# GpSimd's sums behind the last softmax scaling, and the upper half of the scores first, in a graph-network kernel

## The chip, the core and the metric

The kernel runs on one core of one Trainium2 chip. The metric is device time in microseconds (us) of one execution: the median of three runs of the kernel before is 2493.54 us (2493.31 to 2493.93). All data are float32.

The engines are named as in the profile: PE multiplies matrices, DVE (VectorE) and ACT (ScalarE) work element by element, POOL (GpSimd) adds and subtracts whole tiles here, SP issues most of the DMAs. PSUM has eight banks of 128 x 512 float32, into which PE writes.

## The reference, cut to what matters

A graph convolution stands ahead of four transformer layers, and another behind them. The change touches the attention of layers 1 to 3 alone (layers are counted from 0):

```python
xb = xf.reshape(BS, n // BS, d)                      # 16 graphs of 64 nodes, d = 512
q = (xb @ Wq).reshape(BS, -1, H, DH)                 # 8 heads of 64
k = (cond @ Wk).reshape(BS, -1, H, DH)               # 256 keys for each graph
v = (cond @ Wv).reshape(BS, -1, H, DH)
att = jnp.einsum('bnhd,bmhd->bhnm', q, k) * DH ** (-0.5)
w = jax.nn.softmax(att, axis=-1)
o = jnp.einsum('bhnm,bmhd->bnhd', w, v).reshape(BS, -1, H * DH)
...
u = _ln(h, ln3_w[i], ln3_b[i]) @ geglu_w[i] + geglu_b[i]
val, gate = jnp.split(u, 2, axis=-1)
f = val * jax.nn.gelu(gate, approximate=False)
```

## The kernel before, in words

**Products in seven parts.** Each large product is split in 2 x 2 blocks and made from seven block products instead of eight (Strassen's scheme in Winograd's form). It needs sums and differences of blocks of both factors; where these are of weights or inputs they are made on POOL: `sums_of_a`, `sums_of_b` (L213 to L223) and `inner_right` (L969). A PE product then reads a sum as it would read the block.

**Steps.** The attention of a layer goes in eight steps, g = 0 to 7, of two graphs (128 rows) each. In step g the scores of that step are made (`scores`, L755): 16 matmul calls fill four PSUM banks, two for each half `c2` of the heads, a bank holding two heads for each of `a` = 0, 1. Then, for each bank u, DVE takes the row maximum (L774), ACT the exponentials with their sum (L779), DVE the reciprocal (L782) and two in-place scalings of 128 x 256 (L784): eight scalings a step, and `scores.last` is the last of them. While this goes on, PE makes the values of the next step (`values`, L744, by `seven`, L711: products pa, pb, pc, pd, then pa, pc, pd again, whose banks DVE and ACT empty at L722 to L738). Then `mix` (L789) transposes the scaled probabilities (L813), copies them to SBUF as pT (L816 on DVE, L818 on ACT) and multiplies them by the values (L802, bank po).

**Joint keys.** In layers 1 to 3 the keys of steps g + 1 and g + 2 are made together at the end of the odd steps g = 1, 3, 5 (`KeyPair`, L1102). This is a seven-part product whose parts are partly seven-part products again. For the inner ones, `cond_rights` (L1149) makes 16 differences of 128 x 256 on POOL (L973, tiles kr): four for each of four inner products, and the first seven-part product on PE (`seven_of`, L992) reads the first eight, the second one the last eight. `KeyPair.run` writes the keys' four tiles: those of the upper half of the heads (`kT(1, a)`) by DVE in `upper` and `lower` (L1141, L1144), those of the lower half by ACT, in `first` and, behind the very last products, in `final` (L1147). Behind the joint keys comes `scores` of step g + 1, which is even: it takes c2 = 0, the lower half, first.

**First gate weights.** In step 6 of layers 1 to 3 (`g == NG - 2`) POOL makes the four sums of 128 x 1024 for the first quarter of the gated projection (`geglu_weights`, L900; tiles ges, wgate; L220 to L223). Six row blocks of the next normalised input are also turned in this step: 24 transposes tr_ln on PE, whose results DVE (L698) and ACT (L700) scale into place.

**What sets the order.** Each engine takes its instructions in the order of the program; a scheduling layer has made this order and the waits between engines from what each tile is written and read by. `waiting_for(ins, engine)` (L60) adds one more wait: every instruction that is traced inside, on that engine, also waits for `ins`. The sums of the joint keys (L1499) have no such wait: they start when their DMAs have landed and POOL has come to them. The first gate weights of layers 1 to 3 (L1511) wait for `scaled.last`, which is the last normalisation on DVE (L172, tile xn_ln), ahead of the step's scores.

PSUM banks and SBUF tiles are given out in rotation; a bank's new writer waits for its last reader.

Of the kernel before, what the change touches and what calls it, by code (L numbers as in the profile page):

```python
# [23 lines left out]
def gnn_kernel(  # L24
# [67 lines left out]
    def bank(name):  # L92
        return psum.tile([P, 512], F32, tag="bank", name=name)

    def t512(name, dtype=F32):
        return work.tile([P, 512], dtype, tag="t512", name=name)
# [658 lines left out]
    def scores(l, g, qT, kT):  # L755


        c0 = (g % 4) * P
        probs = []
        banks = [bank(f"sc_{l}_{g}_{u}") for u in range(4)]  # L760
        for c2 in range(2):
            for a in range(2):
                for j in range(2):
                    pj = slice(j * DH, (j + 1) * DH)
                    for b in range(2):
                        with tc.issue_after(mix.last.ins) if g else nullcontext():
                            nc.tensor.matmul(  # L767
                                banks[2 * c2 + j][b * NPG:(b + 1) * NPG, a * M:(a + 1) * M],
                                qT[g // 4][c2][pj, a, c0 + b * NPG:c0 + (b + 1) * NPG],
                                kT(c2, a)[pj, b * M:(b + 1) * M], start=True, stop=True)  # L770
        for u in range(4):
            ps3 = banks[u].rearrange("p (a m) -> p a m", a=2)
            nmax = small.tile([P, 2], F32, tag="nmax", name=f"nmax_{l}_{g}_{u}")
            nc.vector.tensor_reduce(nmax, ps3, AX.X, OP.max, negate=True)  # L774
            pr = t512(f"pr_{l}_{g}_{u}")
            pr3 = pr.rearrange("p (a m) -> p a m", a=2)
            tot = small.tile([P, 2], F32, tag="tot", name=f"tot_{l}_{g}_{u}")
            for a in range(2):
                nc.scalar.activation(pr3[:, a, :], ps3[:, a, :], AF.Exp,  # L779
                                     bias=nmax[:, a:a + 1], accum_out=tot[:, a:a + 1])  # L780
            inv = small.tile([P, 2], F32, tag="inv", name=f"inv_{l}_{g}_{u}")
            nc.vector.reciprocal(inv, tot)  # L782
            for a in range(2):
                scores.last = nc.vector.tensor_scalar(pr3[:, a, :], pr3[:, a, :], inv[:, a:a + 1],  # L784
                                                      None, OP.mult)
            probs.append(pr)
        return probs

    def mix(l, g, probs, v, between=lambda: None):  # L789

        oT = t512(f"oT_{l}_{g}")
        po = bank(f"po_{l}_{g}")

        def weigh(c2, pTs):
            for a in range(2):
                c = 2 * c2 + a
                for b in range(2):
                    for m in range(MB):
                        for j in range(2):
                            n0 = c * P + b * NPG  # L800
                            at = (a * MB + m) * P + b * NPG
                            mix.last = nc.tensor.matmul(  # L802
                                po[j * DH:(j + 1) * DH, n0:n0 + NPG],
                                v[b][:, m, c * P + j * DH:c * P + (j + 1) * DH],
                                pTs[j][:, at:at + NPG],
                                start=(m == 0), stop=(m == MB - 1))

        last = None
        for c2 in range(2):
            pTs = []  # L810
            for j in range(2):
                u = 2 * c2 + j
                pt = transposed(probs[u], f"pr_{l}_{g}_{u}")  # L813
                pT = t512(f"pT_{l}_{g}_{u}")
                if j:
                    nc.vector.tensor_copy(pT, pt)  # L816
                else:
                    nc.scalar.copy(pT, pt)  # L818
                pTs.append(pT)
            if last is not None:  # L820
                between()
                weigh(*last)
            last = (c2, pTs)
        weigh(*last)
        nc.vector.tensor_copy(oT, po)
        return oT
# [322 lines left out]
    def cond_rights(l, g):  # L1149

        rooms = slots_of(4, f"kr_{l}_{g}")
        of = conds[l, g], conds[l, g + 1]
        return {i: inner_right(nc.gpsimd, *(x[i][:, k, :] for k in range(2) for x in of), room)
                for i, room in zip(INNER[0] + INNER[1], rooms)}
# [206 lines left out]
    for l in range(L):  # L1361
# [109 lines left out]
        for g in range(NG - 1):  # L1471
            if g == NG - 2:
                if l:
                    take_ln3()
                raw = load_geglu(l, 0)
            if l == 0:
                fetch_cond(g + 2)
            probs = scores(l, g, qT, kTs.pop(g))
            ready = [g - 2, g - 1] if g == NG - 2 else [g - 2] if g > 1 and not l else []

            def between(last_key):
                nonlocal left
                if len(oTs) == 2:
                    blocks = pair_sums(l, g - 2, oTs)
                    oTs.clear()
                    if g == NG - 2:
                        with waiting_for(scores.last, mybir.EngineType.Pool):
                            left = geglu_weights(l, 0, *raw)
                    for _ in attn_out_pair(g - 2, *blocks, wo7,
                                           *(bank(f"{x}_{l}_{g}") for x in ("wab", "wcd"))):  # L1490
                        pass
                ln3_norm(*ready, behind=last_key)
                for nb in ready:
                    add_bias(nb)

            if g in (1, 2):
                fetch_x(2 * l + g - 1)
            if l and g % 2:
                key_rights = cond_rights(l, g + 1)  # L1499

                def kept_moments(ins):
                    if g > 1:
                        with tc.issue_after(ins.ins):
                            moments_into(mv_kept[:, 2 * (g - 3):2 * (g - 1)], [h[g - 3], h[g - 2]],
                                         f"ln3_{l}_{g - 3}")

                vs[g + 1] = values(l, g + 1, wv, beside=kept_moments)
            elif l and g:
                turned = range(g) if g == NG - 2 else []
                if turned:  # L1510
                    with waiting_for(scaled.last, mybir.EngineType.Pool):  # L1511
                        left = geglu_weights(l, 0, *raw)
                vs[g + 1] = values(l, g + 1, wv, late=lambda: [ln3_turn(nb) for nb in turned])
                next_cond(l, g + 2)
                next_cond(l, g + 3)
            else:
                if g or l:
                    kT, vs[g + 1] = kv(l, g + 1, wk, wv, between,
                                       late=lambda: [ln3_turn(nb) for nb in ready])
                else:  # L1520
                    kT, vs[1] = kT_1, values(0, 1, wv)
                kTs[g + 1] = whole(kT)
                save_conds()
                next_cond(l, g + 2)
                if l:
                    next_cond(l, g + 3)
                    spare.append(rows.tile([P, D], F32, tag="last", name=f"spare_{l}"))
                    wk_lefts = inner_lefts(wk, [x[:, i * P:(i + 1) * P] for x in spare
                                                for i in range(4)])
            if g in (1, 2):  # L1530
                base_of(2 * l + g - 1)
            for nb in ready:
                if nb >= 4:
                    ln3_sums(nc.gpsimd, nb)
            oTs.append(mix(l, g, probs, vs.pop(g)))
            if l and g % 2:
                blocks = pair_sums(l, g - 1, oTs)
                oTs.clear()
                pair = KeyPair(l, g + 1, wk, wk_lefts, key_rights, (conds[l, g + 1], conds[l, g + 2]))
                pair.run(scale_kept if g == NG - 3 else lambda: None,  # L1540
                         lambda *banks: attn_out_pair(g - 1, *blocks, wo7, *banks,
                                                      tc.keep_in_program_order))
                if g == NG - 3:
                    ln3_norm(g - 1, g)
                kTs.update({g + 1 + n: pair.of(n) for n in range(2)})
        oT, = oTs
        g = NG - 1
        kT, v = kTs[g], vs[g]
        fT, fS, quads = quads_of(l, 0, left, right)
        probs = scores(l, g, qT, kT)  # L1550
# [133 lines left out]
```

## Time and profile before

| | |
|---|---|
| median of three runs | 2493.54 us |
| the profiled execution | 2493.92 us |
| its span, first to last instruction of the program | 2492.1 us |
| PE busy | 2460.9 us |
| DVE busy | 1574.9 us |
| ACT busy | 691.6 us |
| POOL busy | 807.4 us |
| DMA queue q1, share of 16 engines | 19.0% |

All times inside the program are read against the span, and 1.8 us of the profiled execution lie outside it. A row of the timeline has the start and the duration in us, the engine, the line, the operation, out<-in by the tiles' names, the shape and a count of merged instructions; in brackets stands the idle time of the engine before it and what ended it. The view of stretches has, for each stretch, its length, then for each engine the busy time and in brackets the number of instructions, then PE's granted clock. The view of one line has the minimum, median and maximum duration in ns. PE's ends are modelled and its matmuls overlap, so a step's length is taken from the start of its scores to the start of the next step's.

### The profile page before, as it was taken

The numbers are of one execution on the slowest core, as the hardware profiler recorded it, in microseconds if no ns is written. First come the engines' busy times: TensorE is split into PE (matmuls) and PEld (weight loads), VectorE is DVE, ScalarE is ACT, GpSimd is POOL, SyncE is SP. The second block draws the span as 40 slices with busy tenths as digits, with TensorE's granted clock in tenths as the row PEclk, the third lists the DMA queues.
The fourth block names the chain that finished last, engine by engine and source line by source line (L and its number), as shares of the span: only waits on it lengthen the run. The fifth ranks groups of instructions, "written<-read, shape, count | busy, mean of one in ns | idle before, by whom it ended". The sixth has DMA issues, their size and how long they took to land. (4 is left out here: it accounts for less than half of the span.)

```text
span 2492.1 us, 33980 instructions
## 1 busy us (share of the span) xinstructions
PE 2460.9 (99%) x12968; PEld 1869.3 (75%) x12968; DVE 1574.9 (63%) x3199; ACT 691.6 (28%) x1564; POOL 807.4 (32%) x883
## 2 busy tenths in 40 slices
PE   8999999999999999999999999999999999999999
PEld 5778886677778887577787888477787888577775
DVE  9655665666765657666675667666684566666661
ACT  7322222122213334122212333222222333322221
POOL 0322223632422222532542223344523141444410
PEclk9999999999999999999999999999999999999999
DMA  6313222110312211111212222011121121111110
GB/s 177 132 39 107 98 92 87 51 39 13 102 30 81 94 64 55 39 43 34 98 34 73 73 77 69 23 45 51 34 97 68 40 96 52 51 51 51 51 68 35
DMA packets 70395, 162.97 MB, mean 65 GB/s; under 512 B 5880, under 2 KB 6208, under 8 KB 70224
## 3 DMA queue, kind: packets, MB, share of 16 engines
q1 hardware_dynamic: 68128, 155.28, 19.0%
q0 software_dynamic: 1376, 4.30, 0.5%
q8 instruction: 107, 1.75, 0.3%
q10 hardware_dynamic: 720, 1.11, 0.1%
q14 instruction: 64, 0.52, 0.1%
HBM read 137.60 MB, written 23.07 MB: 64 GB/s over the span
## 5 line engine op out<-in xcount | busy, mean ns | idle before, releaser
L220 POOL TENSOR_TENSOR ges<-wgate,wgate 128x1024 f32<-128x1024 f32 x16 | 37.6, 2352 | 420.8 <-DVE fs L1175 401.3
L779 ACT ACTIVATE pr<-sc,nmax 128x256 f32<-128x256 f32 x256 | 118.0, 474 | 173.7 <-DVE nmax L774 173.7
L302 PE MATMUL pa_v<-wv,ct 128*128 128x256 f32 x512 | 123.8, 384 | 1.7 <-ACT s_v L722 1.7
L302 PE MATMUL pc_v<-wv,ct 128*128 128x256 f32 x512 | 121.6, 380 | 2.6 <-DVE u_v L728 2.4
L302 PE MATMUL fa<-wff,fT 128*128 128x256 f32 x512 | 121.6, 379 | 0.0
L302 PE MATMUL pd_v<-wvs,ct 128*128 128x256 f32 x512 | 121.0, 379 | 0.0
L784 DVE TENSOR_SCALAR pr<-pr,inv 128x256 f32<-128x256 f32 x256 | 115.8, 494 | 2.8
L302 PEld LDWEIGHTS fa<-wff,fT 128*128 128x128 f32 x512 | 97.3, 190 | 21.8 <-issue 9.6
L302 PEld LDWEIGHTS pa_v<-wv,ct 128*128 128x128 f32 x512 | 95.4, 190 | 22.2 <-issue 6.2
L302 PEld LDWEIGHTS pc_v<-wv,ct 128*128 128x128 f32 x512 | 96.2, 190 | 17.5 <-DVE u_v L728 5.0
L1009 ACT COPY gs<-ga 128x512 f32<-128x512 f32 x48 | 27.9, 582 | 287.7 <-PE ga L1002 287.7
L302 PEld LDWEIGHTS pd_v<-wvs,ct 128*128 128x128 f32 x512 | 97.3, 190 | 13.2
L302 PE MATMUL ga<-ln3T,wval 128*128 128x512 f32 x224 | 104.4, 594 | 0.0
L774 DVE TENSOR_REDUCE nmax<-sc 128x2 f32<-128x512 f32 x128 | 82.9, 678 | 33.3 <-PE sc L767 33.3
L1083 ACT ACTIVATE g<-g,gcols 128x512 f32<-128x512 f32 x96 | 69.3, 722 | 94.8 <-DVE g L1080 94.8
L1210 DVE TENSOR_TENSOR hall<-fd,hall 128x512 f32<-128x512 f32 x64 | 44.1, 689 | 54.1 <-PE fd L302 54.1
L1428 POOL TENSOR_TENSOR hall<-hall,ffb 128x512 f32<-128x512 f32 x32 | 40.1, 1276 | 117.5 <-DVE fs L1175 71.2
L302 PE MATMUL gc<-ln3S,wgate 128*128 128x512 f32 x160 | 75.2, 592 | 0.0
L802 PEld LDWEIGHTS po<-pT,v 128*64 128x64 f32 x2048 | 62.9, 138 | 11.7 <-issue 7.2
L802 PE MATMUL po<-pT,v 128*64 128x64 f32 x2048 | 67.7, 224 | 3.5 <-DVE pT L816 3.5
L1210 DVE TENSOR_TENSOR hall<-fc,hall 128x512 f32<-128x512 f32 x64 | 44.0, 687 | 41.6 <-PE fc L302 41.6
L302 PEld LDWEIGHTS ga<-ln3T,wval 128*128 128x128 f32 x224 | 41.3, 190 | 35.9 <-issue 34.4
(476 smaller groups left out, 6146.0 us busy)
## 6 DMA issues: line engine op xcount, KB each, us to landing
ct<-cond_dram SPq DMA_DIRECT2D x72, 512.0 KB, 5.5
wval<-in_L_gnn_geglu_w_dram SPq DMA_DIRECT2D x32, 512.0 KB, 3.8
wgate<-in_L_gnn_geglu_w_dram SPq DMA_DIRECT2D x32, 512.0 KB, 4.6
wff<-in_L_gnn_ffo_w_dram SPq DMA_DIRECT2D x32, 512.0 KB, 3.8
cond_dram<-ct SPq DMA_DIRECT2D x24, 512.0 KB, 3.0
cond<-in_L_gnn_cond_dram SPq DMA_DIRECT2D x32, 256.0 KB, 4.6
ct<-cond_dram SPq DMA_DIRECT2D x24, 256.0 KB, 5.7
wk<-in_L_gnn_Wk_dram SPq DMA_DIRECT2D x8, 512.0 KB, 4.3
```

What stands on the lines that cost most here:

```text
L220: t.tensor_tensor(s1, a21, a22, OP.add)
L302: each(nc.tensor.matmul(at, left[:, k, l0:l1], right[:, k, r0:r1], start=start and n == 0 and k == 0, stop=n == len(cols_of) - 1 and k == ...
L774: nc.vector.tensor_reduce(nmax, ps3, AX.X, OP.max, negate=True)
L779: nc.scalar.activation(pr3[:, a, :], ps3[:, a, :], AF.Exp, bias=nmax[:, a:a + 1], accum_out=tot[:, a:a + 1])
L784: scores.last = nc.vector.tensor_scalar(pr3[:, a, :], pr3[:, a, :], inv[:, a:a + 1], None, OP.mult)
L802: mix.last = nc.tensor.matmul(po[j * DH:(j + 1) * DH, n0:n0 + NPG], v[b][:, m, c * P + j * DH:c * P + (j + 1) * DH], pTs[j][:, at:at + NPG ...
L1009: nc.scalar.copy(s1, a)
L1083: nc.scalar.activation(g, g, AF.Gelu, bias=gate)
L1210: nc.vector.tensor_tensor(to, halves_of(of), to, OP.add)
L1428: nc.gpsimd.tensor_tensor(h[nb], h[nb], ffb, OP.add)
```

## The change

Three things are changed in layers 1 to 3, and nothing elsewhere. The sums for the joint keys wait, on POOL, for the step's last scaling of probabilities (`scores.last`). The sums for the first gate weights wait for it as well, in place of the last normalisation. And `scores` of steps 2, 4 and 6 takes the upper half of the heads first, in the matmuls, in the softmax behind them and in `mix`.

```diff
-        probs = []
+        probs = {}
         banks = [bank(f"sc_{l}_{g}_{u}") for u in range(4)]
-        for c2 in range(2):
+        halves = (1, 0) if l and g and g % 2 == 0 else (0, 1)
+        for c2 in halves:
             for a in range(2):
...
-        for u in range(4):
+        for u in (2 * c2 + j for c2 in halves for j in range(2)):
...
-            probs.append(pr)
+            probs[u] = pr
...
-        for c2 in range(2):
+        for c2 in dict.fromkeys(u // 2 for u in probs):
...
             if l and g % 2:
-                key_rights = cond_rights(l, g + 1)
+                with waiting_for(scores.last, mybir.EngineType.Pool):
+                    key_rights = cond_rights(l, g + 1)
...
                 if turned:
-                    with waiting_for(scaled.last, mybir.EngineType.Pool):
+                    with waiting_for(scores.last, mybir.EngineType.Pool):
                         left = geglu_weights(l, 0, *raw)
```

Line numbers in the text are those of the kernel before. In the built programs, the order on SP is the same in both. On POOL it is the same but for one pair of neighbours inside each set of 16 sums. On PE, DVE and ACT the halves of steps 2, 4 and 6 change places, and nothing else moves. No instruction is added or removed.

## The prediction

> **What bounds the kernel now.** I read the page's busy shares first, then PE's waits, then the durations of DVE's scalings, and last the lengths of the steps.
>
> ```profile
> PE 2460.9 (99%) x12968; PEld 1869.3 (75%) x12968; DVE 1574.9 (63%) x3199; ACT 691.6 (28%) x1564; POOL 807.4 (32%) x883
> PE po L802 <- DVE pT L816: 3.5, 3, 1.2
> PE tr_ln L184 <- DVE u_v L725: 2.7, 3, 0.9
> PE pc_v L302 <- DVE u_v L728: 2.4, 3, 0.9
> PE pa_v L302 <- ACT s_v L722: 1.7, 3, 0.6
> ```
>
> PE is busy in 2460.9 of 2492.1 us. As the change takes no matmul away, only PE's waits can be won, and what adds a wait to PE costs its full length. Four of its waits (total, times, longest) come three times each, once in each of layers 1 to 3, and all four end on work behind DVE's softmax. DVE is busy 63% overall, so something local holds it:
>
> ```profile
> L784 DVE TENSOR_SCALAR pr<-pr,inv x256: 336/349/2507, 177.4 to 2140.0; 128x256 f32<-128x256 f32 x128
> L784 DVE TENSOR_SCALAR pr<-pr,inv x8: 344/348/353, 828.3 to 831.2; 128x256 f32<-128x256 f32 x8
> L784 DVE TENSOR_SCALAR pr<-pr,inv x16: 342/809/885, 846.3 to 899.8; 128x256 f32<-128x256 f32 x16
> 960.55 2.71 DVE L784 TENSOR_SCALAR pr<-pr,inv 128x256 f32<-128x256 f32 x2
> 963.85 4.21 DVE L784 TENSOR_SCALAR pr<-pr,inv 128x256 f32<-128x256 f32 x2
> 969.41 0.68 DVE L725 TENSOR_TENSOR u_v<-pb_v,s_v 128x512 f32<-128x512 f32 x1
> 958.33 2.35 POOL L220 TENSOR_TENSOR ges<-wgate,wgate 128x1024 f32<-128x1024 f32 x1 [4.88 <-DVE xn_ln L172]
> 965.55 2.35 POOL L223 TENSOR_TENSOR ges<-wval,ges 128x1024 f32<-128x1024 f32 x1
> ```
>
> One scaling of 128 x 256 takes 349 ns by the median and up to 2507. In step 2 of layer 1 (from 824), where POOL does nothing, all eight lie within 344 to 353. In steps 3 and 4 (846 to 900) the median of 16 is 809 ns: there POOL's 0.73 us sums for the joint keys run beside them. In step 6 POOL's four gate sums run from 958.33 to 967.90, each 2.35 us, and a pair of scalings takes 2.71 or 4.21 us. So a scaling that falls beside POOL waits for about the rest of the sum that is running. The instructions behind it on DVE, u_v at 969.41 first, are late for PE.
>
> What that costs PE is the length of a step, from the first score to the next step's:
>
> ```profile
> 777.84:824.46 46.62, 46.62 (x305) 40.44 (x301) 26.64 (x50) 14.85 (x36) 7.81 (x11) 1.00 0.06 18
> 842.70:890.35 47.65, 46.88 (x304) 40.35 (x300) 29.95 (x52) 14.14 (x35) 19.29 (x28) 1.00 0.31 106
> 1419.45:1467.02 47.57, 46.89 (x304) 40.35 (x300) 29.87 (x52) 14.14 (x35) 19.30 (x28) 1.00 0.31 106
> 1996.12:2043.91 47.79, 46.89 (x305) 40.35 (x301) 30.09 (x52) 14.14 (x35) 19.31 (x28) 1.00 0.32 105
> 824.46:842.70 18.24, 18.24 (x170) 15.79 (x169) 11.07 (x25) 7.41 (x22) 0.00 (x0) 1.00 0.40 146
> 890.35:908.95 18.60, 18.51 (x169) 15.70 (x168) 12.50 (x23) 6.70 (x21) 9.17 (x13) 1.00 0.00 1
> 2043.91:2062.49 18.58, 18.50 (x169) 15.69 (x168) 12.48 (x23) 6.70 (x21) 9.15 (x13) 1.00 0.00 1
> 955.57:979.92 24.35, 21.72 (x194) 18.45 (x193) 21.58 (x46) 11.01 (x33) 14.41 (x12) 1.00 0.40 132
> 2109.11:2133.44 24.33, 21.71 (x194) 18.45 (x193) 21.57 (x46) 11.00 (x33) 14.39 (x12) 1.00 0.43 131
> ```
>
> The first row is step 1 of layer 1, whose sums ended before its scalings began; PE never pauses in it. Rows two to four are step 3 of layers 1 to 3: the same PE work in 47.57 to 47.79. Then step 2 (clean), step 4 of layers 1 and 3, and step 6 of layers 1 and 3. The granted clock is 1.00 throughout, so nothing here is throttling.
>
> **The change part by part.** *Key sums later.* The wait puts the 16 sums of an odd step behind its own eight scalings. Step 3 then has no POOL beside its softmax, nor has step 4, beside which the sums of step 5 ran. I take the clean steps as what is left:
> - step 3: 47.65, 47.57 and 47.79 less 46.62 is 1.03 + 0.95 + 1.17 = 3.15 us.
> - step 4: 18.60 less 18.24 is 0.36; with layer 3's 0.34, and layer 2 between, 3 x 0.35 = 1.05 us.
> - steps 1 and 5 are clean already: 0.
>
> *What the wait could make late.* Behind the sums on POOL stand only the four sums of pairs of outputs (L850 on), which wait for oT. PE reads the first eight key sums in kb.
>
> ```profile
> 784.10 0.62 DVE L784 TENSOR_SCALAR pr<-pr,inv 128x256 f32<-128x256 f32 x2
> 768.71 0.73 POOL L973 TENSOR_TENSOR kr<-ct,ct 128x256 f32<-128x256 f32 x1 [11.73 <-DMA ct<-cond_dram]
> 778.45 1.52 POOL L973 TENSOR_TENSOR kr<-ct,kr 128x256 f32<-128x256 f32 x2
> 796.72 0.72 POOL L850 TENSOR_TENSOR os<-oT 128x256 f32<-128x256 f32 x1 [16.75 <-DVE oT L825]
> 796.74 0.59 PE L1002 MATMUL kb<-kr,wks 128*128 128x256 f32 x2
> ```
>
> In step 1 the last scaling ends at 784.72. The 16 sums take 768.71 to 779.97 now, 11.3 us, so they will run from 784.7 to 796.0: 0.7 us ahead of L850's own start at 796.72. The first eight are done at about 790.4, 6.3 us before kb at 796.74. The other odd steps have the same distances once their softmax is clean, and DMAs that held the sums until now have landed before. So this costs nothing; no DMA is issued by POOL here, and SP's order is unchanged.
>
> *What the sums fall beside now.* Next on DVE are u_v, v, pT and oT, whose source is PSUM; they ran beside POOL before with no loss (below, the u_v of L728 never over 693 ns). Step 1 also has two additions from SBUF to SBUF:
>
> ```profile
> L728 DVE TENSOR_TENSOR u_v<-pc_v,u_v x32: 680/692/693, 134.8 to 2123.7; 128x512 f32<-128x512 f32 x32
> L1447 DVE TENSOR_TENSOR x_again<-x_again,bias_out x8: 679/681/1446, 213.6 to 1986.3; 128x512 f32<-128x512 f32 x8
> 787.35 0.68 DVE L730 TENSOR_TENSOR v<-pd_v,u_v 128x512 f32<-128x512 f32 x1
> 790.19 1.89 PE L302 MATMUL pd_v<-wvs,ct 128*128 128x256 f32 x8
> ```
>
> L1447 took 1446 ns once, against 681. If it and its neighbour L1448 each take that long, v (L730) ends at 788.03 + 1.53 = 789.56, and PE needs its bank at 790.19. I take 0; without that cover it would be 3 x 1.53 = 4.6 us. [...]
>
> *Gate sums later.* In step 6 the four sums will run behind the last scaling, at about 958.1 + 5.75 = 963.9 (5.75: step 1's first maximum at 778.97 to 784.72), until 973.5. They end before POOL's next work, at 974.77 now, and PE reads them only behind step 7. To see what the step takes without stalls, I add the 24 transposes tr_ln to the clean step 2:
>
> ```profile
> 773.98 1.91 PE L184 MATMUL tr_pr<-ident,pr 128*128 128x128 f32 x16
> 775.82 2.08 PE L802 MATMUL po<-pT,v 128*64 128x64 f32 x64
> 778.97 1.29 DVE L774 TENSOR_REDUCE nmax<-sc 128x2 f32<-128x512 f32 x2 [0.32 <-PE sc L767]
> 974.77 1.44 POOL L213 TENSOR_TENSOR ln3S<-ln3T,ln3T 128x256 f32<-128x256 f32 x2 [6.87 <-DVE ln3T L698]
> ```
>
> Sixteen transposes take 775.82 - 773.98 = 1.84 us, 24 take 2.76: 18.24 + 2.76 = 21.0, and 24.35 - 21.0 = 3.35 us a layer. The idle times agree: 0.6 + 0.9 + 1.2 = 2.7 us, and each pause costs some 0.26 more than its idle time (step 3: 47.65 less 46.62 is 1.03, of which 0.77 is idle by 47.65 less 46.88), 3.4 in all. I take 3 x 3.4 = 10.2 us. DVE turns its 12 halves tr_ln behind u_v and v. These start some 5.5 us sooner (963.9 against 969.41), while PE comes only 3 us sooner, so DVE's lateness should be gone.
>
> *Upper half first.* Behind the joint keys, PE's scores wait within themselves:
>
> ```profile
> 779.72 1.99 PE L302 MATMUL pa_v<-wv,ct 128*128 128x256 f32 x8
> 824.46 2.27 PE L767 MATMUL sc<-kT,qT 64*64 64x256 f32 x32
> 826.65 1.56 PE L302 MATMUL pa_v<-wv,ct 128*128 128x256 f32 x6
> 824.56 0.59 ACT L1147 COPY kT<-kb 128x512 f32<-128x512 f32 x1 [1.14 <-PE kb L1126]
> 820.25 0.69 DVE L1144 TENSOR_TENSOR kT<-kc,kw 128x512 f32<-128x512 f32 x1 [1.30 <-PE kc L1126]
> ```
>
> From the first score to the values it is 826.65 - 824.46 = 2.19 us; in step 1, 779.72 - 777.84 = 1.88 (777.84 from the stretch above). The 0.31 more is the wait for ACT's copy of the last key tile, 824.56 to 825.15. The upper half needs DVE's tiles alone, the last done at 820.94. Taken first, it fills about half of 1.88 us, to 825.4, and then the copy is there. This saves 0.31 in each of nine places: 2.8 us. In the built program the upper half waits, of ACT, only for work ahead of those last copies.
>
> *Sum.* 3.15 + 1.05 + 10.2 + 2.8 = 17.2 us. From the profiled 2493.92 that gives 2476.7; that run lies 0.4 above the median of 2493.54, from which it is **2476.3 us** (0.7% faster).
>
> **The rivals.**
> 1. *Step 6 keeps a stall.* With 12 halves tr_ln and both sets of copies, DVE or ACT may still be late for PE at po; then only half of 10.2 comes: 2481.4. For it: DVE is busy 21.58 of 24.35 us there. Against: two pairs of scalings alone take 2.71 + 4.21 = 6.92 us of that, where two clean pairs take 2 x 0.62, so 5.7 us of DVE's work go. Chance 0.09.
> 2. *The halves gain nothing*, because the second half now waits for the same copy: 2476.3 + 2.8 = 2479.1. Against it: the copy ends a quarter of a microsecond before that half begins. Chance 0.05.
> 3. *The contention stays*: the scalings are slow for another reason than POOL, or the sums still fall beside scalings. Then only the halves pay: 2493.54 - 2.8 = 2490.7. Against it: step 2's eight even scalings. Chance 0.03.
> 4. *PE waits for the key sums* (slower). Place: kb in all nine odd steps, the first reader of kr. It begins when the first eight sums end later than 796.74, that is if they take over 12.0 us instead of 5.65; each microsecond beyond costs 9 us, and slower than before by 0.2% needs 17.2 + 5 = 22.2 us, 2.5 us late at each. Then the sums would take 1.8 us each, where they take 0.73 beside stalled scalings. Price at that point: 2498.5. Chance 0.02.
>
> **How the numbers follow.** The forecast has 0.81. The range reaches down to 2474 (the 0.26 us beyond each idle time come from one step; at twice that, the nine pauses of step 6 give 9 x 0.26 = 2.3 us more), and up to 2481.4, where rival 1, the stalled additions (2476.3 + 4.6 = 2480.9) and rival 2 lie: 2474 to 2481.4. What two runs of this kernel can tell apart is about 0.2%, or 5 us. Faster by more: forecast, rivals 1 and 2, 0.95. Within: rival 3, 0.03. Slower: 0.02.
>
> **What would show it.** Right: scalings of steps 3, 4 and 6 at 0.35 us, no wait of PE on u_v, s_v or pT in layers 1 to 3; step 3 at 46.6, step 4 at 17.9, step 6 at 20.6 us; 1.88 us from score to values everywhere; L1447 up to 1.45 us with no pause of PE behind it. Wrong: PE waiting for kr or os, an idle PE inside step 6, scalings of any step still over 0.5 us, or slower scalings of step 7 beside POOL's ln3S, which the later gate sums may push there.

## The result, and the profile after

The changed kernel takes 2477.08 us (median; 2475.9 to 2477.17), the kernel before 2493.73 us beside it (2493.31 to 2494.58). The ratio is 0.9932, with a 95% interval of 0.9914 to 0.9949: 16.65 us, 0.7%, less. The forecast was 2476.3 us.

The page of the kernel after, its first row:

```profile
PE 2454.0 (99%) x12968; PEld 1865.6 (75%) x12968; DVE 1543.6 (62%) x3199; ACT 692.4 (28%) x1564; POOL 807.9 (33%) x883
```

The instruction counts are those of before, and POOL is as busy as before (807.4 us then). DVE is busy 31 us less for the same 3199 instructions: the profile counts a stalled scaling as busy for its whole time, a median of 809 ns in steps 3 and 4 of layer 1 before, 347 in steps 3 to 6 now.

The stretches of layer 1 in the kernel after: step 1, step 3, step 4 and step 6.

```profile
778.44:825.06 46.62, 46.62 (x304) 40.44 (x300) 27.10 (x50) 14.85 (x36) 17.67 (x24) 1.00 0.06 18
842.99:889.62 46.63, 46.63 (x305) 40.44 (x301) 26.85 (x52) 14.14 (x35) 16.82 (x24) 1.00 0.31 109
889.62:907.55 17.93, 17.93 (x170) 15.44 (x169) 9.87 (x23) 6.70 (x21) 0.00 (x0) 1.00 0.00 1
954.17:974.73 20.56, 20.56 (x194) 18.02 (x193) 16.31 (x46) 11.21 (x33) 12.05 (x8) 1.00 0.47 156
```

In each row the first two numbers, length and PE's busy time, are now equal: PE has no pause left there. Step 3 went from 47.65 to 46.63 us, step 4 from 18.60 to 17.93, step 6 from 24.35 to 20.56, and step 2, which has the halves alone, from 18.24 to 17.93. That is 1.02 + 0.67 + 3.79 + 0.31 = 5.8 us in layer 1, and 5.7 and 5.9 in layers 2 and 3: 17.4 in all. The span shrank by 2492.1 - 2475.4 = 16.7. The rest was lost ahead of these layers, where both kernels are alike: step 1 starts at 778.44 against 777.84.

DVE's scalings in steps 3 to 6 of layer 1 (the line is now L785):

```profile
L785 DVE TENSOR_SCALAR pr<-pr,inv x32: 341/347/354, 846.6 to 962.0; 128x256 f32<-128x256 f32 x32
```

All 32 lie between 341 and 354 ns. Before, those of steps 3 and 4 had a median of 809, and step 6 had some of 2.5 us. All scalings of the kernel after:

```profile
L785 DVE TENSOR_SCALAR pr<-pr,inv x256: 340/348/821, 177.9 to 2123.2; 128x256 f32<-128x256 f32 x128
```

Seven of the 256 are still over 0.5 us: four in layer 0 (700 to 821 ns) and one in step 0 of each of layers 1 to 3 (630 to 633 ns). All seven lie where nothing was changed, and the same seven were as slow before (700 to 819 and 632 to 633 ns). In PE's waits over the whole kernel after, the four rows of before (on pT, on the two u_v and on s_v, three times each) are gone.

The key sums of step 1 in the kernel after, on POOL, with PE's first reader and DVE's two additions of x_again:

```profile
785.40 0.73 POOL L974 TENSOR_TENSOR kr<-ct,ct 128x256 f32<-128x256 f32 x1 [27.81 <-DVE pr L785]
786.08 0.73 POOL L974 TENSOR_TENSOR kr<-ct 128x256 f32<-128x256 f32 x1
786.76 1.18 POOL L974 TENSOR_TENSOR kr<-ct,kr 128x256 f32<-128x256 f32 x1
787.91 1.17 POOL L974 TENSOR_TENSOR kr<-ct,ct 128x256 f32<-128x256 f32 x1
...
795.91 1.52 POOL L974 TENSOR_TENSOR kr<-ct,kr 128x256 f32<-128x256 f32 x2
797.39 0.72 POOL L851 TENSOR_TENSOR os<-oT 128x256 f32<-128x256 f32 x1
```

```profile
786.63 0.73 DVE L1448 TENSOR_TENSOR x_again<-x_again,bias_out 128x512 f32<-128x512 f32 x1
787.39 1.10 DVE L1449 TENSOR_TENSOR x_again<-x_again,again 128x512 f32<-128x512 f32 x1
788.41 0.68 DVE L730 TENSOR_TENSOR v<-pd_v,u_v 128x512 f32<-128x512 f32 x1
```

```profile
790.79 1.89 PE L302 MATMUL pd_v<-wvs,ct 128*128 128x256 f32 x8
...
797.34 0.59 PE L1003 MATMUL kb<-kr,wks 128*128 128x256 f32 x2
```

The bracket of the first row says that the sums now wait for DVE's scaling (L785). They collide with the two additions instead: two sums take 1.18 and 1.17 us in place of 0.73, and the second addition 1.10 in place of 0.69. DVE's v (L730) still ends at 789.09, 1.7 us ahead of pd_v, where PE needs that bank. The pair sums os start at 797.39, right behind the last key sum: the 0.7 us of room that was forecast is used up by the collision, and PE does not feel it.

The scores behind the joint keys, at the start of step 2 in the kernel after:

```profile
825.06 1.96 PE L768 MATMUL sc<-kT,qT 64*64 64x256 f32 x32
825.17 0.58 ACT L1148 COPY kT<-kb 128x512 f32<-128x512 f32 x1 [1.14 <-PE kb L1127]
826.95 0.48 PE L302 MATMUL pa_v<-wv,ct 128*128 128x256 f32 x1
```

From the first score to the values it is 826.95 - 825.06 = 1.89 us, as forecast, and 2.19 before. ACT's copy of the last key tile now runs beside the first half of the scores.

### The profile page after: what moved, and what is told of

It reads as the page before. It is cut to its first block, busy times and chain, and to the rows that moved or that the text cites. A ratio compares the mean times of both kernels' runs of the same rounds, so it can differ in the third digit from the quotient of the medians.

```text
span 2475.4 us, 33973 instructions
## 1 busy us (share of the span) xinstructions
PE 2454.0 (99%) x12968; PEld 1865.6 (75%) x12968; DVE 1543.6 (62%) x3199; ACT 692.4 (28%) x1564; POOL 807.9 (33%) x883
## 5 line engine op out<-in xcount | busy, mean ns | idle before, releaser
L974 POOL TENSOR_TENSOR kr<-ct,ct 128x256 f32<-128x256 f32 x36 | 27.7, 769 | 245.5 <-DVE pr L785 245.5
L785 DVE TENSOR_SCALAR pr<-pr,inv 128x256 f32<-128x256 f32 x256 | 81.2, 359 | 2.9
```

The lines of the kernel that those rows point to most:

```text
L974: t.tensor_tensor(to, of, less, OP.subtract)
```

## The experiments

The theory: DVE's in-place scalings stall behind the POOL sum that runs beside them, DVE's later tiles are then late, and PE pauses for those. The rivals: the stall has another cause than POOL, or the later sums are late for PE, or only the halves pay. Lines in the rows are each kernel's own.

### The key sums alone

```diff
             if l and g % 2:
-                key_rights = cond_rights(l, g + 1)
+                with waiting_for(scores.last, mybir.EngineType.Pool):
+                    key_rights = cond_rights(l, g + 1)
```

> The kernel before with one part of the change: only the sums for the joint keys wait for the step's last scaling. Theory (a scaling on DVE waits for the GpSimd sum that runs beside it): scalings of steps 3 and 4 at 0.35 us, step 3 at 46.6 us in layers 1 to 3, step 4 at 18.24, step 6 unchanged at 24.3; 4.2 us less than before, about 2489.5. Rival (the scalings are slow for another reason, such as DMA traffic or ACT): they stay at 0.8 us in steps 3 and 4, and the time stays within 1 us of before. Rival (the later sums hold PE back): waits of PE on kr, a step 1 or 5 longer than 46.6, and a time over 2493.7.

Measured: 2489.61 us against 2493.38 before on the same chip, ratio 0.9984 (0.9975 to 0.9993): 3.8 us less. Its steps 3, 4 and 6 of layer 1, and its scalings of steps 3 and 4:

```profile
841.57:888.19 46.62, 46.62 (x304) 40.44 (x300) 26.86 (x52) 14.15 (x35) 16.84 (x24) 1.00 0.32 107
888.19:906.43 18.24, 18.24 (x169) 15.79 (x168) 9.87 (x23) 6.71 (x21) 0.00 (x0) 1.00 0.00 1
953.06:977.41 24.35, 21.70 (x193) 18.44 (x192) 21.59 (x46) 11.03 (x33) 14.41 (x12) 1.00 0.41 132
```

```profile
L784 DVE TENSOR_SCALAR pr<-pr,inv x16: 341/348/354, 845.2 to 895.0; 128x256 f32<-128x256 f32 x16
```

Steps 3 and 4 have the lengths of the clean steps to 0.01 us, the scalings are clean, and step 6 is as before. Both rivals fall: moving POOL's sums and nothing else cures the scalings of exactly the steps that lose POOL, and PE waits for no sum.

### The first gate sums alone

```diff
                 if turned:
-                    with waiting_for(scaled.last, mybir.EngineType.Pool):
+                    with waiting_for(scores.last, mybir.EngineType.Pool):
```

> The kernel before with one part of the change: only the first gate sums wait for the last scaling of step 6. Theory: scalings of step 6 at 0.35 us, step 6 at 20.9 us in place of 24.3, steps 3 and 4 unchanged; 10.4 us less than before, about 2483.3. Rival (step 6 keeps a stall, because DVE and ACT are late with the turned blocks anyway): step 6 at 22 to 23 us, 2487 to 2490. Rival (another reason than GpSimd): no change.

Measured: 2483.95 us against 2493.38, ratio 0.996 (0.9947 to 0.9974): 9.4 us less. Steps 3 and 6 of layer 1:

```profile
842.56:890.50 47.94, 46.89 (x305) 40.36 (x301) 30.24 (x52) 14.14 (x35) 19.30 (x28) 1.00 0.31 108
955.72:976.58 20.86, 20.86 (x194) 18.36 (x193) 16.32 (x46) 11.22 (x33) 12.27 (x9) 1.00 0.48 154
```

Step 6 falls to 20.86 us without a pause, 3.5 less than 24.35, in each of three layers: 10.4 in all. The medians show 1 us less of this than the steps; the profiled execution, with a span of 2482.0 us for 2492.1, shows 10.1. The rival of a stall that stays falls. Step 3 is at 47.94 here and was at 47.65 before with nothing changed in it: what a stalled step costs varied by some 0.3 us between these runs, a clean one (46.62 and 46.63 in the runs here) by 0.01.

### The upper half first alone

```diff
-        for c2 in range(2):
+        halves = (1, 0) if l and g and g % 2 == 0 else (0, 1)
+        for c2 in halves:
...
-        for u in range(4):
+        for u in (2 * c2 + j for c2 in halves for j in range(2)):
```

(and `probs` and `mix` as in the change)

> The kernel before with one part of the change: only the upper half of the scores first behind joint keys, both waits as before. Theory: 1.89 us from the first score to the values in all nine places instead of 2.19; 2.8 us less than before, about 2490.9. Rival (the gain comes only with the waits, since PE would then stand at the slow softmax 0.31 us longer): the idle time of PE in steps 4 and 6 grows by what the scores save, and the time is that of before, but for the three places of step 2: 0.9 us less.

Measured: 2492.9 us against 2493.38, ratio 0.9997 (0.9988 to 1.0006): no gain that can be told from none. Its steps 2, 4 and 6 of layer 1, and two of PE's waits over the whole kernel (total, times, longest):

```profile
824.39:842.32 17.93, 17.93 (x169) 15.44 (x169) 11.07 (x25) 7.41 (x22) 0.00 (x0) 1.00 0.40 144
...
890.29:908.88 18.59, 18.19 (x169) 15.35 (x168) 12.79 (x23) 6.70 (x21) 9.16 (x13) 1.00 0.00 1
955.50:979.84 24.34, 21.39 (x193) 18.10 (x193) 21.58 (x46) 11.00 (x33) 14.40 (x12) 1.00 0.41 132
```

```profile
PE pc_v L302 <- DVE u_v L728: 3.8, 6, 1.1
...
PE pa_v L302 <- ACT s_v L722: 2.6, 3, 0.9
```

Step 2, where nothing stalls, is 0.31 us shorter. Steps 4 and 6 keep their lengths of before, 18.59 and 24.34 us, though PE is through its scores 0.31 us sooner: in both, PE's busy time is 0.32 or 0.33 us less (18.19 for 18.51, 21.39 for 21.72) and its pauses are as much longer. The waits show where it goes. That on u_v (L728) has three new places of some 0.4 us, in step 4, and that on s_v grew from 1.7 to 2.6 in all. So the three steps 2 alone gain, 3 x 0.31 = 0.9 us. As long as DVE's stalled softmax sets the end of a step, PE's earlier start is given back at the next wait.

### Both waits, without the halves

The kernel after with one line edited:

```diff
-        halves = (1, 0) if l and g and g % 2 == 0 else (0, 1)
+        halves = (0, 1)
```

> The changed kernel without the upper half first: both waits alone. Theory: the sum of the two parts, 4.2 + 10.4 = 14.6 us less than before, about 2479.1, with 2.19 us from the first score to the values in nine places, and 2.8 us behind the changed kernel shown in the same way. Rival (parts that overlap): more than 1 us away from the sum of the two single parts.

Measured: 2478.85 us against 2493.38, ratio 0.9941 (0.9927 to 0.9954): 14.5 us less. Steps 2, 3, 4 and 6 of layer 1:

```profile
824.56:842.80 18.24, 18.24 (x169) 15.78 (x168) 11.07 (x25) 7.41 (x22) 0.00 (x0) 1.00 0.39 142
842.80:889.42 46.62, 46.62 (x304) 40.44 (x300) 26.86 (x52) 14.14 (x35) 16.82 (x24) 1.00 0.32 110
889.42:907.66 18.24, 18.24 (x169) 15.78 (x168) 9.88 (x23) 6.70 (x21) 0.00 (x0) 1.00 0.00 1
954.28:975.14 20.86, 20.86 (x193) 18.36 (x192) 16.33 (x46) 11.22 (x33) 12.26 (x9) 1.00 0.49 154
```

No step has a pause. Against the kernel after, steps 2 and 4 are 0.31 longer (18.24 for 17.93) and step 6 is 0.30 (20.86 for 20.56): with the stalls gone, the halves are worth the whole 0.31 us in all nine places, 2.8 us. By the medians it is 16.65 - 14.5 = 2.1 us, from kernels measured beside two different sets of runs of before.

### The key sums later still: behind the values

The kernel after, in which the key sums wait for the last copy of the values (L738) in place of the last scaling:

```diff
-        seven(f"v_{l}_{g}", of_v(wv, conds[l, g]), v11, v12, v21, v22, s1, **also)
+        values.last = seven(f"v_{l}_{g}", of_v(wv, conds[l, g]), v11, v12, v21, v22, s1, **also)
...
-                with waiting_for(scores.last, mybir.EngineType.Pool):
-                    key_rights = cond_rights(l, g + 1)
...
                 vs[g + 1] = values(l, g + 1, wv, beside=kept_moments)
+                with waiting_for(values.last, mybir.EngineType.Pool):
+                    key_rights = cond_rights(l, g + 1)
```

> The changed kernel with the key sums later still: they wait for the last copy of the next step's values (L738), about 8.7 us behind the last scaling. Theory: the first inner product reads in kb the seventh sum first of those that matter, which would then end about 0.6 us late in each of the nine odd steps; some 5 us more than the changed kernel, about 2482, with PE waiting for kr. Rival (the sums still have room, 6.3 us by the prediction's count less 8.7, partly made up by other slack behind kb): no wait on kr, the same time as the changed kernel. Rival (as the prediction's count of eight sums has it): 8.7 - 6.3 = 2.4 us late nine times, 21.6 us, about 2498.6.

Measured: 2482.84 us against 2493.86, ratio 0.9954 (0.9937 to 0.997); its profiled execution has a span of 2481.7 us, 6.3 more than the kernel after. First and seventh of its 16 sums in step 1 on POOL, then PE's first readers, then PE's row for this wait over the whole kernel:

```profile
793.33 0.73 POOL L974 TENSOR_TENSOR kr<-ct,ct 128x256 f32<-128x256 f32 x1 [35.96 <-DVE v L738]
...
797.46 0.71 POOL L974 TENSOR_TENSOR kr<-ct,kr 128x256 f32<-128x256 f32 x1
```

```profile
797.12 0.59 PE L1003 MATMUL kb<-kr,wks 128*128 128x256 f32 x2
798.22 0.70 PE L1003 MATMUL kb<-kr,wvs 128*128 128x256 f32 x2 [0.50 <-POOL kr L974]
```

```profile
PE kb L1003 <- POOL kr L974: 4.2, 9, 0.5
```

PE takes the first sums without a pause and waits at its second reader, for the seventh sum, which ends at 798.17. In the kernel after the sums start at 785.40, the seventh ends at 791.13 and that reader starts at 797.77. So the sums can come 6.6 us later before PE feels it, and what counts is not the end of the first eight but that of the seventh. Here they begin 7.9 us later, without the two slow sums beside the additions (0.9 us), and PE pauses 0.5 us in each of nine places. The odd steps are 0.72 to 0.77 us longer (47.39, 47.34 and 47.34 for 46.62), 2.2 us in each layer and 6.6 in all: a pause costs some 0.25 us beyond its idle time, as in the steps of before.

### The key sums after the outputs

The same, with the wait on the copy of oT (L825 of the kernel before), which is the last thing that `mix` does:

```diff
-        nc.vector.tensor_copy(oT, po)
+        mix.copied = nc.vector.tensor_copy(oT, po)
...
             oTs.append(mix(l, g, probs, vs.pop(g)))
+            if l and g % 2:
+                with waiting_for(mix.copied, mybir.EngineType.Pool):
+                    key_rights = cond_rights(l, g + 1)
```

> The changed kernel with the key sums behind the copy of oT (L825), about 12.5 us behind the last scaling. Theory: another 3.7 us later than behind the values, all of it PE's: 4.3 us in each of nine odd steps, 38 us more than the changed kernel, about 2515; PE idle in front of kb in all nine. Rival (only the first inner product waits and the time is given back later in the joint keys, since DVE and ACT are behind PE there): 20 us or less.

Measured: 2535.6 us against 2493.86, ratio 1.0165 (1.0148 to 1.0182): slower than the kernel before. PE's two waits in step 1 and their sum over the kernel; then short stretches of steps 1, 3 and 5 of layer 1 and of step 1 of layer 2 in which the granted clock (the third number from the right) falls and comes back:

```profile
799.07 1.05 PE L1003 MATMUL kb<-kr,wks 128*128 128x256 f32 x2 [1.95 <-POOL kr L974]
801.79 1.22 PE L1003 MATMUL kb<-kr,wvs 128*128 128x256 f32 x2 [1.67 <-POOL kr L974]
802.80 1.06 PE L1003 MATMUL kc<-kr,wk 128*128 128x256 f32 x2
```

```profile
PE kb L1003 <- POOL kr L974: 34.5, 18, 2.0
```

```profile
799.00:799.50 0.50, 0.43 (x2) 0.33 (x2) 0.00 (x0) 0.00 (x0) 0.50 (x2) 0.78 0.00 0
...
803.00:805.00 2.00, 2.00 (x7) 1.55 (x6) 0.93 (x2) 0.00 (x0) 2.00 (x4) 0.50 0.00 0
805.00:807.00 2.00, 2.00 (x8) 1.71 (x7) 1.08 (x2) 0.00 (x0) 2.00 (x4) 0.72 0.00 0
...
870.00:871.00 1.00, 0.70 (x2) 0.30 (x2) 0.00 (x0) 0.00 (x0) 1.00 (x3) 0.98 1.01 414
...
942.50:943.50 1.00, 0.00 (x0) 0.00 (x0) 0.00 (x0) 0.00 (x0) 1.00 (x2) 0.57 0.28 107
...
1392.70:1393.70 1.00, 0.50 (x1) 0.50 (x2) 0.00 (x0) 0.00 (x0) 1.00 (x2) 0.75 0.00 0
```

This is the fourth rival: here PE waits for the sums in all nine odd steps, twice in each. The waits add up to 34.5 us, yet the kernel is 41.7 us slower than before where the changed one is 16.65 faster: 58.4 us between them, where 38 were expected. The rest stands mostly in the granted clock. A stretch at 0.50 and 1.00 shows by its mean where the change lies: in step 1, 0.78 in 799.00 to 799.50 puts the fall at 799.28, and 0.72 in 805 to 807 the return at 806.12, 6.84 us later. Steps 3 and 5 give 870.96 to 877.80 (0.80 in 877 to 879) and 942.64 to 949.48 (0.63 in 948 to 950), again 6.84 each. In steps 3 and 5 of layers 2 and 3 the falls last as long (in step 3 two matmuls take 0.60 us again from 1468.30 and from 2058.84); the mean clock of the whole execution is 0.988. In step 1 of these two layers the clock falls only as the second pause ends, at 1393.20 and 1983.70 (0.85 in 1983 to 1984), and is back 3.42 us later, at 1396.62 (0.69 in 1396 to 1397) and 1987.12 (0.94 in 1987 to 1988). At half clock two matmuls take 1.06 us, where they take 0.59 otherwise. In the seven long falls some 1.8 of the 6.84 us are the second pause, and PE works in the other 5; in the two short ones it works nearly throughout. It loses half of the time that it works: 7 x 2.5 + 2 x 1.7 = 20.9. With the 34.5 that makes 55.4; with 0.25 us more for each of 18 pauses, as above, it makes 59.9. The measured 58.4 lies between.

### The scalings on another engine

The kernel before, with the scalings of steps 3, 4 and 6 of layers 1 to 3 made by ACT, and POOL's sums left where they were:

```diff
             for a in range(2):
-                scores.last = nc.vector.tensor_scalar(pr3[:, a, :], pr3[:, a, :], inv[:, a:a + 1],
-                                                      None, OP.mult)
+                if l and g in (3, 4, 6):
+                    scores.last = nc.scalar.mul(pr3[:, a, :], pr3[:, a, :], inv[:, a:a + 1])
+                else:
+                    scores.last = nc.vector.tensor_scalar(pr3[:, a, :], pr3[:, a, :],
+                                                          inv[:, a:a + 1], None, OP.mult)
```

> The kernel before, its sums as early as before, but in steps 3, 4 and 6 of layers 1 to 3 the scalings are done by ACT instead of DVE. Theory (only DVE's work from SBUF to SBUF is held up by GpSimd): ACT's scalings take one length of about 0.4 to 0.5 us whether a sum runs beside them or not, DVE's u_v and pT come in time, and PE's waits in these steps go but for 0.2 to 0.4 us where ACT's copy s_v stands behind the scalings; 2479 to 2484. Rival (the sums' traffic in SBUF slows any engine): ACT's scalings take 0.8 us in steps 3 and 4 and over 1.5 us in step 6, and the time is that of before or worse.

Measured: 2480.98 us against 2493.86, ratio 0.9949 (0.9932 to 0.9966): 12.9 us less. Its scalings on ACT, and its steps 3, 4 and 6 of layer 1:

```profile
L785 ACT ACTIVATE pr<-pr,inv x72: 504/518/547, 845.1 to 2108.9; 128x256 f32<-128x256 f32 x72
```

```profile
841.85:888.47 46.62, 46.62 (x305) 40.44 (x301) 24.97 (x44) 17.15 (x43) 18.98 (x28) 1.00 0.32 110
888.47:906.71 18.24, 18.24 (x170) 15.78 (x169) 7.98 (x15) 9.76 (x29) 8.93 (x13) 1.00 0.00 1
953.33:975.01 21.68, 21.13 (x194) 18.27 (x193) 14.42 (x38) 14.21 (x41) 14.83 (x12) 1.00 0.48 148
```

POOL works in all three stretches nearly as in the kernel before (18.98, 8.93 and 14.83 us for 19.29, 9.17 and 14.41), and yet steps 3 and 4 are clean to 0.01 us. All 72 scalings lie within 504 to 547 ns. So neither the time at which POOL works nor the memory traffic of its sums is what slows the softmax; it is that DVE's scalings and POOL's sums meet. That is the theory, by a way that does not touch POOL. DVE's scalings took up to 2507 ns beside POOL and 341 to 354 without, ACT's at most 547 beside it. Why DVE's are held up there and ACT's are not, no run shows. Of PE's four waits only that on s_v is left, 1.7 us in three places: step 6 keeps 0.55 us of idle behind s_v, which ACT now reaches later because its own scalings stand before it.

## Why the prediction was right

**Steps 3 and 4** (3.15 and 1.05 us forecast). Right: the kernel with the key sums alone has them at 46.62 and 18.24 us in all three layers, the clean steps to 0.01 us. The whole was 3.8 us by the medians for 4.2 by the steps.

**Steps 1 and 5** (nothing). Right in time; the working had two slips that the spare time absorbed. The first eight sums were named as the limit, with 6.3 us of room. The limit is the seventh sum, as the late version showed, with 6.6. The second slip is the 0.7 us of room ahead of the pair sums: all of it went into the collision with x_again. Counted from the start of step 1, os starts at 18.95 us (797.39 - 778.44) for 18.88 before (796.72 - 777.84), without effect.

**The two additions of x_again** (0 taken; 1.53 us more forecast as the worst, with 0.63 us of room left even then, 789.56 to 790.19). The collision came, in a smaller size and alike in all three layers: the second addition takes 1.10 us for 0.69, and two of POOL's sums beside them 1.18 and 1.17 for 0.73. DVE's v keeps 1.7 us of room. Both additions are longer than before, but the first by 0.05 us only. The rows show the size: here an instruction loses nearly what the other engine's instruction still has to run when it starts. The first addition starts 0.18 us before the end of the second sum (786.81) and loses 0.05. The third sum, the second addition and the fourth sum each start 0.55 to 0.60 us before the end of the other's and lose 0.41 to 0.45. So, by this working, beside sums of 0.73 us an addition does not lose the 0.77 us that the worst case gave it. That figure came from a row of 1446 ns, at 252.38 in the kernel before, beside a POOL instruction of 1.27 us.

**Step 6** (10.2 us). Right: 24.34 - 20.86 = 3.48 in each layer by the kernel with the gate sums alone, 10.4 in all. No stall stays, so rival 1 falls. The 3.35 from the clean step 2 and 24 transposes was 0.13 short.

**Upper half first** (2.8 us). Right for this change: 17.93 for 18.24 and 20.56 for 20.86. Rival 2 falls: from the first score to the values it is 1.89 us, with ACT's copy beside the first half. But rival 3 was priced wrongly. It gave the halves 2.8 us in a kernel that keeps its stalls, as if the terms of the sum were independent. The halves alone took 0.5 us by the medians, and 0.9 by the steps: in two of three places the earlier score was waited away at the next stalled tile. The right price of rival 3 was 2493.54 - 0.9 = 2492.6.

**The sum.** 3.15 + 1.05 + 10.4 + 2.8 = 17.4 us by the steps, for 17.2 forecast. The median came out 0.8 us above the forecast. In the profiled executions the steps account for it: 17.4 us were won in them and 0.6 lost ahead of step 1, where nothing was changed and the kernels differ by up to 1.7 us (776.7 to 778.4).

**The signs.** Those of being right came, and of those of being wrong only one, by its wording: scalings "of any step" over 0.5 us. The seven that are left lie in layer 0 and in steps 0, which the change does not touch, and PE waits nowhere on the softmax or on the tiles that DVE makes behind it.

**Rival 4.** Its mechanism is real, its place and its point of beginning were about right, and its price was too low. It gave 9 us for each microsecond of lateness; the late versions paid 16.65 - 11.0 = 5.6 us for 4.2 us of pauses, and 58.4 for 34.5, most of the difference through the clock.

## What to carry to other kernels

An engine that is not the bottleneck can slow the one that feeds the bottleneck (DVE's scalings in steps 3 and 4 took a median of 809 ns beside POOL, 348 without): compare the same instruction in steps with and without the neighbour at work, and move the neighbour, or hand the instruction to an engine that it does not hold up (ACT's scalings took at most 547 ns beside POOL). What such a move is worth is the length of the step less that of a clean one; savings inside a step that still waited for something else were given back at that wait (0.9 us of 2.8 were left), so test parts together as well as alone. Before a sum is made later, find the single tile that its reader takes last without pausing: behind that point a microsecond of PE's waits cost 1.3 us here (5.6 for 4.2), and 1.7 where the clock fell as well (58.4 for 34.5).

## What the runs showed of the hardware

**Behind some pauses of 1.9 us and more the clock fell to half, behind others it did not.** In the version with the sums behind oT the clock fell from 1.00 to 0.50 in steps 1, 3 and 5 of layer 1 behind a single pause of 1.9 us, before the second was over. The fall came 0.21 us behind the pause in step 1 (799.07 to 799.28) and 0.77 in step 3 (870.19 to 870.96). Each of the three lasted 6.84 us. The falls in step 1 of layers 2 and 3 lasted 3.42 and came only as the second pause of 2.02 us ended; behind the first, of 1.95 us, two matmuls still took 0.70 us. In the kernel after, ahead of its layers, two pauses of like length went differently (timeline, then stretches):

```profile
26.74 2.40 PE L463 MATMUL hw_in<-w_in,h0T 128*128 128x512 f32 x4 [2.18 <-ACT h0T L455]
...
86.61 1.96 PE L302 MATMUL pa_kT<-ct,wk 128*128 128x256 f32 x8 [2.16 <-DVE v_deg L134]
```

```profile
28.00:29.00 1.00, 1.00 (x3) 0.17 (x2) 1.00 (x7) 1.00 (x3) 0.00 (x0) 0.59 0.97 150
...
87.00:88.00 1.00, 1.00 (x7) 0.87 (x6) 0.83 (x6) 0.00 (x0) 0.00 (x0) 1.00 0.00 0
```

Behind the pause of 2.18 us the clock falls (0.59 in this microsecond, so at 28.18; 0.60 in 30 to 32, so it is back at 31.60, 3.42 us later), behind that of 2.16 it stays at 1.00. In the kernel before it is the other way round: behind the pause ahead of hw_in (2.05 us, to 26.47) the clock stays at 1.00, and behind that ahead of pa_kT (2.20 us, to 85.31) it falls at 86.62 (0.81 in 86 to 87) and is back at 90.04 (0.99 in 90 to 92), again 3.42 us later. Behind the pause of 3.5 us ahead of pc, at the start of the program, it stays at 1.00 in both kernels (to 9.79 before, to 9.82 after). So the length of a pause alone does not decide; what does, and where a limit lies, was not shown, as no run varies one pause alone. In the long fall of step 1 the clock is at 0.50 ahead of the second pause (1.67 us, 800.12 to 801.79) and still at 0.50 behind it, until 806.12. The pause of 0.5 us in step 1 of the late version (1.00 in 798 to 802), and those of up to 1.2 us in layers 1 to 3 of the kernel before (1.00 in the stretches of steps 3, 4 and 6), left the clock at 1.00.

**The collision holds up both sides.** Beside each other, DVE's scalings of 349 ns took up to 2507, and POOL's sums of 0.73 us took up to 1.18 beside the x_again additions. What is lost goes, in the four rows at 786 to 789, with what the other's instruction still has to run: 0.05 us for 0.18, 0.41 to 0.45 for 0.55 to 0.60.
